# First attention of a fused cross-attention kernel: four pools become six, in another order

## The chip, the cores and the metric

The kernel runs on one core of one Trainium2 chip. The metric is the device time of one execution in microseconds (us), lower is better. A core has five instruction streams that matter here: TensorE (PE, matrix products; its weight loads are listed apart as PEld), VectorE (DVE), ScalarE (ACT), GpSimd (POOL) and SyncE (SP), which issues the DMAs. Each stream is executed in the order in which it was written when the program was built; between streams there are only semaphores.

## The reference, cut to what matters

`x` is (8, 112, 512), the context `ctx` (8, 375, 512), all float32. Four layers follow each other on `x`:

```
layer 0:  q = x Wq^T; k = ctx Wk^T; v = ctx Wv^T
          x = x + alpha * (softmax(q k^T / sqrt(512)) v) Wo^T
layer 1:  RWKV block: layer norm, token shift, mixing, a scan over time, group norm, gate, channel mix
layer 2:  a second RWKV block
layer 3:  two cross attentions to ctx with 16 heads of 128 and a 2048-wide GELU MLP, layer norm before each
```

The values of the third layer, `ctx wv`, depend on `ctx` and weights only. Nothing of layers 0 to 2 enters them.

## The kernel before

All activations lie with channels on the 128 partitions: `x` is one tile of 128 x 4 x 896. The program is written with a tile framework. A **pool** is a range of on-chip memory with a stack discipline: pools opened later lie above those still open, and a pool opened after others were closed takes their place from the bottom. What is put into a new pool waits until the pools that lay at its addresses are done with. PSUM, the accumulators of PE, consists of eight banks and is handed out by the same stack. The order of the instructions on each engine is made at build time by a list scheduler: it takes the instructions in the order of the program, and where the next one of an engine is not ready by its own estimate of the times, it puts a later one that is ready first. Only the time loop of the RWKV layers has an order written out by hand.

**Layer 0 (`layer0`, from line 224).** The weights are folded: `w_qk` is made from `w_q` and `w_k` (`turned`, `product`, L305), `q0 = x w_qk` is projected for all tokens (L308), and `w_vo` is made from `w_v` and `w_o` (L315). Then a loop over the eight batches (L316): `context(b)` loads the transposed context tile `cx` (24 KB-per-partition slots for four of them); `park` (L248, every second batch) makes sums and differences of two contexts and stores them to DRAM as `blocks`; `rows` are transposes of `cx` by `ident` (L327); scores `sc` (L333), softmax, transposed probabilities `pt` (L337), and `av` (L343), copied to the tile `z` (L346). At the end one projection, `z` by `w_vo`, is added to `x` (L348 to L352; PE at L161, the eviction `add` on DVE at L350, out of two PSUM banks).

Its pools, bottom first: `a0` (`keep`: `ident`, three `turned` tiles, `w_qk`, `q0`, `z0`, `w_vo`), `a0w` (`work`: `cx`, `blocks`, `rows`, small tiles), and in PSUM `a0p` (`ps`: two banks `mm`, for all projections and transposes of rows) and `a0s` (`ps2`: two banks each of `sc`, `pt`, `av`).

**What comes after.** When layer 0 closes its pools, these are opened, bottom first: `values` (L1429; seven weight tiles `wv`, five context blocks `cv`, six result tiles `k`, two more), `mmp` in PSUM (two banks), `rc` with a short-lived `rs` above it (constants of the RWKV layers: `heads`, `same`, `ident_rs`, `ones_t`, `pick`, L796 to L815), then `r1` and `m1` (first RWKV layer, with six PSUM banks `mp1`). In bytes per partition, worked out from the shapes: `values` 54 KB, `rc` with `rs` 4 KB, `r1` 56 KB, `m1` 30 KB; in layer 0, `ident` 0.5, `turned` 24, `w_qk` 8, `q0` 14, `z0` 14, `w_vo` 8, `cx` 23.4 KB.

**The filler.** `values()` (L820) is a generator of PE work that depends on nothing in the RWKV layers: the values of layer 3, by a seven-product scheme (k1, k6, k7, k2, k8 and two late ones, k5 and k9). Each product is two matmuls of 128 x 512, which the profile lists as four records (`ps_vk`, L906); ACT copies the bank out (L931, L999, L1013), POOL adds for three of the seven (L932), SP stores to DRAM. The first call (`fill(1)`, L1434) issues the loads: four of `cv` (L890), four of `wv` (L839), biases (L950, L951), and four sums of `wv` on POOL (L846 to L849). Later calls of `fill(n)` in the RWKV layers each place n products. Before the time loop of the first RWKV layer these are 3 + 2 + 2 + 2 + 2 inside `mixes(0, ...)` and 8 in `time_mix`.

**The first layer norm of layer 1** (`layer_norm_half`, L166, half 0 of the tokens): partial sums on DVE (`part_mean_ln`, L178, L180), a PE product with a constant matrix (`mean_ln`, L182), the subtraction (`xa`, L187, DVE), squares (L189, ACT), partial sums (`part_var_ln`), PE (`var_ln`, L182), the root (L194, ACT), the reciprocal (L195, DVE), the scaling (L196, DVE; L202, ACT), then the token shift on POOL (`sx`, L359, L360), `xx` on DVE (L438) and the first product of the layer, `ps_t` (L447, PE).

Of the kernel before, what the change touches and what calls it, by code (L numbers as in the profile page):

```python
# [22 lines left out]
F32 = mybir.dt.float32  # L23
# [3 lines left out]
PSUM = bass.MemoryType.PSUM  # L27
ORDERED = {mybir.EngineType.PE, mybir.EngineType.DVE, mybir.EngineType.Activation, mybir.EngineType.Pool}

P = 128  # L30
B, L, C, S = 8, 112, 512, 375
N = B * L
NC = C // P
# [75 lines left out]
def tile_kernel(ctx: ExitStack, tc: tile.TileContext, d: dict, out: bass.AP):  # L109
# [14 lines left out]
    def weight(name, g=None):  # L124

        w = wpool.tile([P, NC, C], F32, tag="w", name=f"w_{name}_{g}")
        nc.sync.dma_start(w, d[name] if g is None else d[name][g])
        return w
# [23 lines left out]
    def mm(ps, name):  # L152
        return ps.tile([P, 512], F32, tag="mm", name=name)

    def project(ps, w, rhs, evacuate, name, hs=(0, 1), os=range(NC)):

        for h in hs:
            for o in os:
                p = mm(ps, f"ps_{name}_{o}_{h}")[:, :NH]
                for k in range(NC):  # L160
                    nc.tensor.matmul(  # L161
                        p, w[:, k, o * P : (o + 1) * P], rhs(k, h), start=k == 0, stop=k == NC - 1
                    )
                evacuate(o, h, p)
# [59 lines left out]
    def layer0():  # L224

        with (
            tc.tile_pool(name="a0", bufs=1) as keep,
            tc.tile_pool(name="a0w", bufs=2) as work,  # L230
            tc.tile_pool(name="a0p", bufs=2, space=PSUM) as ps,
            tc.tile_pool(name="a0s", bufs=2, space=PSUM) as ps2,
        ):
            ident = identity(keep, "a0")
            w_q, w_k = weight("L0_xattn_w_q"), weight("L0_xattn_w_k")
            nc.sync.dma_start(x, d["xT"])
            cxs = {}

            def context(b):
                cxs[b] = work.tile([P, NC, S], F32, tag="cx", name=f"cx0_{b}", bufs=4)  # L240
                nc.sync.dma_start(cxs[b], d["ctxT"][:, b])

            context(0)
            w_v, w_o = weight("L0_xattn_w_v"), weight("L0_xattn_w_o")
            nc.sync.dma_start(alpha, d["alpha"].to_broadcast([P, 1]))
# [37 lines left out]
            def turned(w, name):  # L283

                t = keep.tile([P, NC, C], F32, tag="turned", bufs=3, name=f"t_{name}")
                for o in range(NC):
                    p = mm(ps, f"ps_t{name}_{o}")
                    for k in range(NC):
                        nc.tensor.transpose(p[:, k * P : (k + 1) * P], w[:, k, o * P : (o + 1) * P], ident)
                    (nc.vector.tensor_copy if o % 2 else nc.scalar.copy)(t[:, o, :], p)  # L290
                return t

            def product(a, b, name, scale=1.0):

                y = keep.tile([P, NC, C], F32, tag=name, name=name)
                for c in range(NC):
                    p = mm(ps, f"ps_{name}_{c}")
                    for k in range(NC):
                        nc.tensor.matmul(
                            p, a[:, k, c * P : (c + 1) * P], b[:, k, :], start=k == 0, stop=k == NC - 1  # L300
                        )
                    nc.scalar.activation(y[:, c, :], p, AF.Copy, scale=scale)
                return y

            w_qk = product(turned(w_q, "q"), turned(w_k, "k"), "w_qk", 1.0 / math.sqrt(C))  # L305
            q = keep.tile([P, NC, N], F32, name="q0")
            z = keep.tile([P, NC, N], F32, name="z0")
            project(  # L308
                ps,
                w_qk,  # L310
# [1 line left out]
                lambda o, h, p: nc.scalar.copy(halves(q[:, o, :], h), p),  # L312
                "q0",
            )
            w_vo = product(turned(w_v, "v"), w_o, "w_vo")  # L315
            for b in range(B):  # L316
                tok = slice(b * L, (b + 1) * L)
                if b + 1 < B:
                    context(b + 1)
                cx = cxs[b]  # L320
# [1105 lines left out]
    shared["spill"] = ctx.enter_context(tc.tile_pool(name="spill", bufs=1, space=bass.MemoryType.DRAM))  # L1426
    shared["blocks"] = shared["spill"].tile([P, (UNITS + 3) * BLOCKS * BLOCK], F32, name="blocks")
    layer0()
    with (  # L1429
        tc.tile_pool(name="values", bufs=1) as shared["pool"],  # L1430
# [80 lines left out]
```

## Time and profile before

| | us |
|---|---|
| median of 3 runs | 2971.14 (2968.95 to 2975.28) |
| the profiled execution, its own time | 2968.51 |
| its span on the core | 2966.1 |
| PE busy | 2861.6 (96% of the span) |
| DVE busy | 1610.9 (54%) |
| ACT busy | 998.9 (34%) |
| POOL busy | 876.4 (30%) |
| mean granted clock of PE | 0.988 of full speed |

A line of the timeline is: start in us, duration, engine, line of the program, operation, output <- inputs, and in brackets how long the engine had been idle before it and what released it. A line of the chain is: start, duration, engine, what and line; the chain is followed back from the last instruction to what released each step, and "issue" is time in which the engine waited for nothing that the profile shows. A line of the stages is: from:to, length, then busy time and number of instructions of PE, PEld, DVE, ACT and POOL, the granted clock of PE as a share of full speed, the busy share of the DMA engines and the GB/s that they moved. "SPq" is SP's queue of DMA issues.

### The profile page before, as it was taken

What the parts mean: (1) busy time and instruction counts of PE and PEld (TensorE: products, weight loads), DVE (VectorE), ACT (ScalarE), POOL (GpSimd) and SP (SyncE); (2) the same over time, 40 slices, a digit from 0 to 9 for tenths busy, and PEclk for the clock granted to TensorE, in tenths of its full rate; (3) what the DMA queues carried; (4) which work ended last, traced back from release to release, by engine and by line L of the source; (5) the groups of instructions that cost most, each with busy time, mean ns of one, the idle gap of its engine ahead of it and who ended that gap; (6) DMA issues with size and microseconds to landing.
All of it is one profiled execution on the core that took longest, in us unless ns stands there. A gap on an engine that the chain in (4) does not pass through costs nothing.

```text
span 2966.1 us, 29798 instructions
## 1 busy us (share of the span) xinstructions
PE 2861.6 (96%) x10130; PEld 1561.7 (53%) x10130; DVE 1610.9 (54%) x2350; ACT 998.9 (34%) x1992; POOL 876.4 (30%) x702
## 2 busy tenths in 40 slices
PE   8979999999999999999899999999999999999999
PEld 4734443344444433356465666666565656656544
DVE  1563288857342688743455554545554554545455
ACT  2123355533233555532332323232331323323311
POOL 2142078754231588732411010100302010000030
PEclk9989999999999999999999999999999999999999
DMA  6421398944321889742344344334233433432110
GB/s 255 150 89 45 116 291 247 282 135 126 96 68 54 246 251 271 225 141 70 130 130 128 129 128 129 108 119 140 88 120 102 144 108 119 140 114 77 42 54 25
DMA packets 199318, 402.90 MB, mean 136 GB/s; under 512 B 33288, under 2 KB 119592, under 8 KB 192384
## 3 DMA queue, kind: packets, MB, share of 16 engines
q1 hardware_dynamic: 199168, 401.01, 43.0%
q8 instruction: 81, 1.33, 0.2%
q14 instruction: 69, 0.57, 0.1%
HBM read 323.16 MB, written 77.91 MB: 135 GB/s over the span
## 4 chain that ended last, share of the span: by engine, by line
PE 80%; DVE 7%; POOL 4%; issue 3%; ACT 3%; DMA 2%; SPq 0%; DVEq 0%; POOLq 0%; ACTq 0%
PE ps_vk L906 13%; PE ps_k1k L1134 10%; PE ps_k5k L1134 7%; PE av L1303 6%; PE sc L1290 5%; PE ps_o L161 3%; PE pt L1293 3%; PE ps_fk L161 2%; PE ps_k1q L1061 2%; PE ps_k L484 2%; PE ps_r L484 2%; PE ps_k5q L1061 2%; PE ps_k7q L1061 2%; PE ps_fr L161 2%; PE ps_k5o L1061 1%
## 5 line engine op out<-in xcount | busy, mean ns | idle before, releaser
L906 PE MATMUL ps_vk<-wv,cv 128*128 128x512 f32 x1328 | 597.0, 600 | 29.5 <-DMA wv<-in_L_xattn_wv 8.2
L906 PEld LDWEIGHTS ps_vk<-wv,cv 128*128 128x128 f32 x1328 | 249.3, 191 | 361.7 <-issue 301.8
L932 POOL TENSOR_TENSOR k<-k,k 128x512 f32<-128x512 f32 (+1 forms) x153 | 201.7, 1318 | 306.7 <-ACT k L931 261.6
L691 DVE TENSOR_TENSOR_SCAN st<-decay,kv 128x904 f32<-128x904 f32 x128 | 260.7, 2037 | 16.7 <-POOL rs L695 4.0
L695 POOL TENSOR_TENSOR rs<-st,r 128x896 f32<-128x896 f32 x128 | 246.7, 1928 | 55.3 <-DVE st L691 42.4
L218 ACT ACTIVATE prob<-sc,top 112x376 f32<-112x376 f32 (+1 forms) x264 | 151.8, 575 | 322.6 <-DVE top L215 195.2
L1303 PEld LDWEIGHTS av<-pts,v 125*128 125x128 f32 (+1 forms) x1536 | 185.7, 193 | 31.0 <-DVE pts L1299 16.0
L1290 PE MATMUL sc<-k,q 128*112 128x376 f32 x512 | 201.1, 485 | 0.7 <-ACT prob L218 0.7
L1283 POOL COPY k<-over_k 128x4 f32<-128x4 f32 x64 | 13.8, 224 | 604.7 <-PE sc L1290 576.7
L1303 PE MATMUL av<-pts,v 125*128 125x112 f32 (+1 forms) x1536 | 190.0, 278 | 1.8 <-DVE pts L1299 0.9
L1134 PE MATMUL ps_k1k<-cs,wsk 128*128 128x375 f32 x480 | 178.6, 481 | 1.5 <-ACT p1k L1137 1.5
L215 DVE TENSOR_REDUCE top<-sc 112x1 f32<-112x376 f32 (+1 forms) x264 | 143.5, 545 | 64.3 <-PE sc L1290 51.9
L687 DVE TENSOR_TENSOR kv<-vp,k 128x904 f32<-128x904 f32 x128 | 141.5, 1105 | 64.8 <-ACT vp L589 59.0
L931 ACT COPY k<-ps_vk 128x512 f32<-128x512 f32 (+1 forms) x153 | 89.2, 583 | 183.1 <-PE ps_vk L906 180.2
L999 ACT COPY k<-ps_vk 128x512 f32<-128x512 f32 (+1 forms) x153 | 89.1, 582 | 153.6 <-PE ps_vk L906 148.7
L1293 PEld LDWEIGHTS pt<-ident_l,prob 112*125 112x125 f32 (+1 forms) x768 | 97.8, 176 | 72.0 <-DVE prob L220 43.9
L1293 PE MATMUL pt<-ident_l,prob 112*125 112x112 f32 (+1 forms) x768 | 121.4, 277 | 2.5 <-DVE prob L220 1.9
L220 DVE TENSOR_SCALAR prob<-prob,total 112x376 f32<-112x376 f32 (+1 forms) x264 | 118.3, 448 | 8.0
L1134 PEld LDWEIGHTS ps_k1k<-cs,wsk 128*128 128x128 f32 x480 | 89.5, 190 | 59.4 <-ACT p1k L1137 1.8
L589 ACT COPY vp<-vj 128x896 f32<-128x896 f32 x124 | 112.8, 910 | 7.0 <-DMA vj<-rows 3.1
L1141 DVE TENSOR_TENSOR k<-ps_k5k,u2k 128x375 f32<-128x375 f32 x52 | 28.5, 548 | 159.2 <-PE ps_k5k L1134 158.2
L1310 DVE TENSOR_TENSOR ctxt<-av,bv 128x448 f32<-128x448 f32 x64 | 39.9, 624 | 128.8 <-PE av L1303 128.8
(384 smaller groups left out, 4800.6 us busy)
## 6 DMA issues: line engine op xcount, KB each, us to landing
vj<-rows SPq DMA_DIRECT2D x124, 448.0 KB
cv<-blocks SPq DMA_DIRECT2D x181, 251.5 KB
cs<-blocks SPq DMA_DIRECT2D x120, 375.0 KB
wvs<-k SPq DMA_DIRECT2D x128, 256.0 KB
v<-wvs SPq DMA_DIRECT2D x64, 512.0 KB
cx<-in_ctxT SPq DMA_DIRECT2D x38, 750.0 KB
v<-wvs SPq DMA_DIRECT2D x64, 252.0 KB
wvs<-k SPq DMA_DIRECT2D x64, 224.0 KB
```

The source lines that it names most:

```text
L161: nc.tensor.matmul(p, w[:, k, o * P : (o + 1) * P], rhs(k, h), start=k == 0, stop=k == NC - 1)
L215: nc.vector.tensor_reduce(top, scores, AX.X, ALU.max, negate=True)
L218: nc.scalar.activation(prob, scores, AF.Exp, bias=top, accum_out=total)
L691: nc.vector.tensor_tensor_scan(flat(st), flat(decay[:, c]), flat(kv), 0.0, ALU.mult, ALU.add)
L695: nc.gpsimd.tensor_mul(by_batch(rs), st[:, :, :L], by_batch(r[:, c, :]))
L906: nc.tensor.matmul(to, left, right, start=start and n == 0, stop=k == 1, skip_group_check=True)
L932: nc.gpsimd.tensor_add(y, z, y)
L1061: nc.tensor.matmul(to, lhsT, rhs, start=start and k == 0, stop=k == 1, skip_group_check=not start)
L1134: nc.tensor.matmul(y, lhsT, rhs, start=start and k == 0, stop=k == 1, skip_group_check=True)
L1290: nc.tensor.matmul(sc, q[:, o, tok], kt[:, o, :], start=True, stop=True)
L1293: nc.tensor.transpose(pt[t][:nt, o, :], prob[:, t0 : t0 + nt], ident[:L, :L])
L1303: nc.tensor.matmul(av[:, o, :], v[:nt, t, o * HD : (o + 1) * HD], pts[:nt, t, o, :], start=t == 0, stop=t == 2,)
```

## The change

Layer 0 takes six pools instead of four, and their order changes. The context tiles `cx` leave `work` for a pool of their own, `a0c` (`near`), which is opened before `keep`. `z0` and `w_vo` leave `keep` for a pool `a0z` (`last`), opened after `keep`. In PSUM the pool with `sc`, `pt` and `av` (`a0s`) is opened first, the one with the two `mm` banks (`a0p`) last. `product` gets the pool as an argument. No instruction is added, removed or given other operands than other addresses.

```diff
         with (
+
+            tc.tile_pool(name="a0s", bufs=2, space=PSUM) as ps2,
+            tc.tile_pool(name="a0c", bufs=4) as near,
             tc.tile_pool(name="a0", bufs=1) as keep,
+            tc.tile_pool(name="a0z", bufs=1) as last,
             tc.tile_pool(name="a0w", bufs=2) as work,
             tc.tile_pool(name="a0p", bufs=2, space=PSUM) as ps,
-            tc.tile_pool(name="a0s", bufs=2, space=PSUM) as ps2,
         ):
...
-                cxs[b] = work.tile([P, NC, S], F32, tag="cx", name=f"cx0_{b}", bufs=4)
+                cxs[b] = near.tile([P, NC, S], F32, tag="cx", name=f"cx0_{b}")
...
-            def product(a, b, name, scale=1.0):
+            def product(a, b, name, pool, scale=1.0):
 
-                y = keep.tile([P, NC, C], F32, tag=name, name=name)
+                y = pool.tile([P, NC, C], F32, tag=name, name=name)
...
-            w_qk = product(turned(w_q, "q"), turned(w_k, "k"), "w_qk", 1.0 / math.sqrt(C))
+            w_qk = product(turned(w_q, "q"), turned(w_k, "k"), "w_qk", keep, 1.0 / math.sqrt(C))
             q = keep.tile([P, NC, N], F32, name="q0")
-            z = keep.tile([P, NC, N], F32, name="z0")
+            z = last.tile([P, NC, N], F32, name="z0")
...
-            w_vo = product(turned(w_v, "v"), w_o, "w_vo")
+            w_vo = product(turned(w_v, "v"), w_o, "w_vo", last)
```

## The prediction

> **What bounds the kernel now.** The page says PE 96% busy, so time is to be had only where PE waits. I read the busy time by stage first, cut at the end of layer 0's last projection, at the landing of the values' weights and at the first product of layer 1.
>
> ```profile
> core 0: us, PE busy (x) PEld busy (x) DVE busy (x) ACT busy (x) POOL busy (x), PEclk, DMA share, GB/s
> 134.00:146.00 12.00, 12.00 (x34) 6.09 (x33) 3.82 (x6) 0.53 (x1) 0.00 (x0) 1.00 0.56 133
> ...
> 158.30:166.40 8.10, 0.02 (x1) 0.06 (x1) 3.90 (x4) 1.70 (x1) 0.00 (x0) 0.66 0.94 293
> 166.40:176.00 9.60, 7.28 (x11) 3.00 (x12) 5.98 (x4) 2.98 (x4) 8.10 (x4) 0.75 0.40 136
> 176.00:186.40 10.40, 6.87 (x17) 2.55 (x15) 8.51 (x12) 4.77 (x9) 6.14 (x9) 0.93 0.39 126
> ```
>
> For 8.1 us PE does nothing and the DMA engines are 94% busy; just before, in the last projection, PE is full and POOL idle. The same question put to 186.4 to 260 and 260 to 390 gives PE 68.5 of 73.6 and 128.5 of 130 us: after the gap PE is the bound again.
>
> Then who waited for whom, from 140 to 190 us:
>
> ```profile
> POOL ident_rs masks.py:197 <- PE ps_o L161: 48.5, 1, 48.5
> ...
> PE ps_vk L906 <- DMA wv<-in_L_xattn_wv: 8.2, 1, 8.2
> ...
> PE ps_t L447 <- DVE xx L438: 3.5, 1, 3.5
> ...
> PE ps_vk L906 <- POOL wv L848: 2.3, 1, 2.3
> ```
>
> The three PE lines add to 14.0 us, all of PE's waiting here. Why the loads are late, SP's queue says:
>
> ```profile
> 142.94 0.63 SPq L409 DMA_DIRECT2D d<-in_L_xattn_decay_w  x1
> 157.54 1.79 SPq L890 DMA_DIRECT2D cv<-blocks  x4
> 159.38 2.64 SPq L839 DMA_DIRECT2D wv<-in_L_xattn_wv  x4
> ```
>
> SP is idle for 14 us and starts when the projection's last product ends (157.47). By the sizes `cv` lies at 28 to 38 KB, over `w_qk` and `q0`, last read at 127.6 by the scores. So the wait is for the whole pool `keep`, whose `z0` and `w_vo` are read to the end. Last the chain of waits (130 to 190 us):
>
> ```profile
> 134.16 23.33 PE ps_o L161 x62
> ...
> 159.38 6.91 DMA wv<-in_L_xattn_wv
> ...
> 166.38 2.05 PE ps_vk L906 x2
> 168.42 1.51 PE var_ln L182 x2
> ...
> 170.61 2.67 DVE part_mean_ln L180
> ...
> 175.88 2.94 DVE rstd__ln L195
> ...
> 181.04 1.94 DVE xa L196
> ...
> 186.35 4.10 PE ps_t L447 x5
> ```
>
> The layer norm's `var_ln` stands in PE's order behind a value product that waits for its weights; then DVE is late for the reciprocal.
>
> **What the change does to the waits.** `near` (23.4 KB) and `keep` without `z0` and `w_vo` (46.5 KB) are 69.9 KB; `values` with `rc` and `rs` takes 58 KB and lies inside them. Their last reader is the last transpose of `pt` by `ident`, ending at 130.6. So the values' loads, their POOL sums and the constants of the RWKV layers can start at about 131 instead of 157.5. In PSUM, by the stack, the values' two banks now lie over `sc`, free by then, and the layer norm's six over `pt`, `av` and the projection's two `mm` banks.
>
> **Part by part**, on the profiled execution.
>
> *Loads.* From the first issue at 157.54 to the last sum's operands 10 us passed (POOL starts at 167.66). Issued at 131 they land near 141, or up to 9 us later, at 150, if the 1.5 MB of layer 1's own loads (issued 134.6 to 143.6, which is their 9 us) come between. The 18 issues of this group (4 `cv`, 4 `wv`, 4 biases, 1 `heads`, 4 `same`, 1 `first`) take SP 10.5 us. They move ahead of or between layer 1's 14 small loads, which are wanted by `ps_t`, 30 us later: nothing.
>
> *`var_ln`.* Its input is ready at 162.86 + 1.28 = 164.14, it starts at 168.22: 4.08 us. Its two records take 1.70 us at the low clock after the idle stretch, 0.92 for `mean_ln`: 0.78 us.
>
> *Reciprocal.* Its input is ready at 171.29 + 0.63 = 171.92, it starts at 175.88: 3.96 us. In between DVE does two sums for half 1 (L180), 2.65 us each instead of 0.62 at 162.86, while POOL does the sums of `wv`. With POOL's sums gone they take 1.3 us, in the shadow of the root.
>
> *Small work in DVE's order.* The reciprocal ends at 178.82, `xa` starts at 180.97, behind L952, L804 and L813, which need late loads: 2.15 us. They go into the projection, where DVE is busy 3.5 to 3.8 of 12 us.
>
> *A new wait.* `mean_ln` (157.31 before) takes a bank of a pool that now covers the `mm` banks; if it waits for the last eviction (L350, 157.51 to 158.19), as the pool-wide wait above suggests, it ends at 159.1 instead of 158.2. Behind it on PE stand value products that can as well be put before it; DVE's `xa` waits. Between 0 and 0.9 us; I take 0.9, since SP's wait was of that kind.
>
> The sum: 4.08 + 0.78 + 3.96 + 2.15 - 0.9 = 10.1 us earlier for `ps_t`: 176.3. Step by step: `mean_ln` to 159.1, `xa` to 161.3, squares to 163.0, sums to 165.0, `var_ln` to 166.0, table and root to 168.0, reciprocal to 170.95, `xa` to 172.95, and 3.4 us to `ps_t` as before (182.97 to 186.35).
>
> *The gap as room for products.* From 158.2 to 176.3 are 18.1 us, less 1.84 for the two norm products 16.3. The six products (24 records) that ran there took 11.0 us at full clock (start to start 0.456 us, 16 in 7.30) and fit. Of the other 5.3 us the scheduler may fill up to two more products of 1.8 us, if ACT, which has the squares, the root and 0.58 us a copy to do, keeps up: 0 to 3.6, I take 1.8. It counts, since PE is the bound afterwards. Against it, a product may stand before `var_ln` when that is ready: 0 to 1.8, I take 0.9. Together 10.1 + 1.8 - 0.9 = **11 us**.
>
> *POOL's sums beside the projection.* Their 10.3 us now lie at about 141 to 152, beside evictions (L350) that must keep pace with PE: 2.94 us a bank, two banks. Here a rule speaks against the change: the Trainium skill, "SBUF — State Buffer", section "Who interferes with whom", says that a DVE instruction with two SBUF inputs and a GpSimd instruction that reads SBUF lock each other out for a whole instruction. The L180 row agrees (2.65 against 0.62). Counting `alpha` as the second SBUF input, each of four evictions would lose about 2 us, 8 in all less a bank's slack of 2.9: 5 us. But L459 has that form (PSUM, a column, an SBUF operand) and takes 0.67 us at 204.4 to 206.2 with POOL busy throughout. So only the three `part_mean` sums are blocked, at most 2 us each, one per bank time: 0.68 + 2.65 = 3.3 us against 2.94, which the spare bank absorbs. I take 0; bounds 0 to 5.
>
> *All else* is the same instructions in the same layer: nothing. What could still move is the written order further down, since the scheduler sees other ready times. The trace can't price that; the nearest row for a bad guess is the 8.2 us wait for `wv`. I give it no sign and keep 3 us either way in the range.
>
> The median is 2.6 us above the profiled execution (2971.14, 2968.51); I take the gain off the median: 2971.1 - 11 = 2960.
>
> **The rivals.** What a measurement of this kernel can tell from no change is 0.2%, 5.9 us: 2965.2 to 2977.1.
>
> *A, the forecast:* gap closed as summed. 2953 to 2965; chance 0.66.
>
> *B, half given back:* POOL's sums do hold up evictions (5 us), or products stand before both norm products (up to 2 x 1.8): 11 - 5 = 6, or with both 2. 2965 to 2969; chance 0.16. For it speaks the L180 row; against it L459.
>
> *C, it doesn't do what it says:* some instruction still ties `near` or `keep` to the end of the projection. Then nothing moves: 2971, within 3. Against: every reader of `cx`, `q0` and `ident` that the trace shows ends by 130.6. Chance 0.07.
>
> *D, slower:* a value product is written into PE's order inside the projection, before its weights have landed. For it: in the trace of before PE stood at `ps_vk` from 158.23 and the weights came at 166.38, so the order assumed them at least 8 us too early. Issued at 131 beside layer 1's loads they land as late as 150; PE standing from 139 to 150 would lose 11 us, the whole gain, and the products done there no longer fill the layer norm's gap: five of them at 1.8 are 9 us. So -11 + 11 + 9: 2980. With the gap left empty it is slower than before from a wait of 2 us on, by over 0.2% from 8. Against it: PE has the projection's products ready and full from 134 (12.00 of 12.00), and these come first in the program. Chance 0.11.
>
> **The numbers.** Faster by over 0.2%: A but for its edge, and half of B: 0.72. Within: the rest of B, C and some of D: 0.18. Slower: 0.10. Range 2953 to 2969: A and B, 0.82.
>
> **What would show it.** SP's `cv` and `wv` issues at 131 to 135; POOL L846 to L849 before 155 with PE's `ps_o` still in 23.5 us (else B); no wait of PE for DMA `wv`; L180 at 0.62; `ps_t` at 176 and the granted clock near 1 from 158 to 176. I am wrong if the issues stay at 157, if `ps_o` stretches, or if `ps_t` comes 10 us earlier and the end does not: then a later stage has its own bound.

## The result and the profile after

| | before | after |
|---|---|---|
| median of 7 runs each, us | 2970.40 (2966.97 to 2975.28) | 2961.31 (2951.97 to 2963.65) |
| ratio, 95% interval | | 0.9968 (0.9957 to 0.9979) |
| profiled execution, its own time, us | 2968.51 | 2963.03 |
| its span, us | 2966.1 | 2961.2 |

The change is 9.1 us faster by the medians; 2960 was forecast. In a second set on one chip (22 runs of the change, 49 of before) it was 2959.85 against 2967.23, ratio 0.9982 (0.9972 to 0.9992). By the ratios, which are not quotients of the medians, the gain is 9.5 us (6 to 13) in the first set and 5.3 us (2 to 8) in the second. That it is faster is clear; its size is known to some us only, since single runs of one kernel spread over 15 us and more (2959.99 to 2978.88 for before in that set).

SP's queue in the changed kernel (lines from L300 on stand 3 higher):

```profile
132.81 2.02 SPq L893 DMA_DIRECT2D cv<-blocks  x4
134.89 2.25 SPq L842 DMA_DIRECT2D wv<-in_L_xattn_wv  x4
...
154.88 0.64 SPq L398 DMA_DIRECT2D maa<-in_L_xattn_maa_w  x1
```

The loads leave when the last transpose of `pt` ends, 25 us earlier than before, and layer 1's own loads now come after them. PE's timeline from there to the first product of layer 1:

```profile
132.56 0.93 PE L161 MATMUL ps_o<-z,w_vo 128*128 128x448 f32 x2
133.42 2.90 PE L346 MATMUL av<-pts,rows 125*128 125x112 f32 x24
136.16 14.46 PE L161 MATMUL ps_o<-z,w_vo 128*128 128x448 f32 x38
153.93 9.29 PE L161 MATMUL ps_o<-z,w_vo 128*128 128x448 f32 x24 [3.31 <-DVE x L353]
163.05 1.02 PE L909 MATMUL ps_vk<-wv,cv 128*128 128x512 f32 x2
163.99 1.02 PE L182 MATMUL mean_ln<-part_mean_ln,mean_c 128*128 128x448 f32 x2
164.84 6.48 PE L909 MATMUL ps_vk<-wv,cv 128*128 128x512 f32 x14
171.16 0.92 PE L182 MATMUL var_ln<-part_var_ln,mean_c 128*128 128x448 f32 x2
172.00 9.71 PE L909 MATMUL ps_vk<-wv,cv 128*128 128x512 f32 x22
182.99 1.02 PE L450 MATMUL ps_t<-xx,maa 128*128 128x448 f32 x2 [1.28 <-DVE xx L441]
```

The layer norm's gap is almost full of value products, with no wait for DMA; the only stand left is 1.28 us for `xx`. But inside the last projection there is a new stand: PE waits 3.31 us for an eviction. Where it comes from, DVE's and POOL's timelines of the same stretch show:

```profile
142.26 2.35 POOL L849 TENSOR_TENSOR wv<-wv,wv 128x1024 f32<-128x1024 f32 x1 [8.84 <-DMA wv<-in_L_xattn_wv]
142.35 2.73 DVE L178 TENSOR_TENSOR part_mean_ln<-x 128x448 f32<-128x448 f32 x1
144.69 2.61 POOL L850 TENSOR_TENSOR wv<-wv,wv 128x1024 f32<-128x1024 f32 x1
145.01 0.67 DVE L353 SCALAR_TENSOR_TENSOR x<-ps_o,alpha,x 128x448 f32<-128x448 f32 x1
145.72 2.06 DVE L180 TENSOR_TENSOR part_mean_ln<-part_mean_ln,x 128x448 f32<-128x448 f32 x1
147.37 2.62 POOL L851 TENSOR_TENSOR wv<-wv,wv 128x1024 f32<-128x1024 f32 x1
147.70 5.58 DVE L955 TENSOR_TENSOR over<-over,bv 4x512 f32<-4x512 f32 x2
150.07 2.67 POOL L852 TENSOR_TENSOR wv<-wv,wv 128x1024 f32<-128x1024 f32 x1
...
153.20 0.67 DVE L353 SCALAR_TENSOR_TENSOR x<-ps_o,alpha,x 128x448 f32<-128x448 f32 x1
```

Before, with POOL idle in the projection, the same partial sums and, later, the same bias differences took:

```profile
140.19 0.63 DVE L178 TENSOR_TENSOR part_mean_ln<-x 128x448 f32<-128x448 f32 x1
143.20 0.62 DVE L180 TENSOR_TENSOR part_mean_ln<-part_mean_ln,x 128x448 f32<-128x448 f32 x1
178.74 1.78 DVE L952 TENSOR_TENSOR over<-over,bv 4x512 f32<-4x512 f32 x2
```

The eviction itself takes 0.67 us at 145.01 with POOL busy. The work with two inputs in on-chip memory that stands ahead of it in DVE's order is what POOL holds up: two partial sums take 2.73 and 2.06 us in place of 0.63 and 0.62, and the two bias differences 5.58 us in place of 1.78. Experiment 5 tests this. The stages, cut at these points:

```profile
136.00:150.60 14.60, 14.60 (x41) 7.21 (x40) 9.58 (x7) 0.53 (x1) 8.10 (x4) 1.00 0.54 183
150.60:154.00 3.40, 0.09 (x2) 0.08 (x1) 3.40 (x4) 0.00 (x0) 2.13 (x1) 1.00 0.06 12
...
163.20:171.20 8.00, 8.00 (x20) 3.06 (x19) 4.58 (x5) 3.36 (x4) 1.19 (x3) 1.00 0.56 150
171.20:183.00 11.80, 10.52 (x26) 4.26 (x24) 8.08 (x6) 8.07 (x13) 5.20 (x7) 1.00 0.45 133
```

PE is full in the layer norm's first 8 us, the stretch in which it had done nothing, and the granted clock is 1.00 throughout.

Since layer 0 reaches the projection at another time in every run (129.1 to 134.6 us among the profiled ones, 2.2 us later here than before), the steps below are compared from the projection's first product on PE. From there, in us:

| | before | after | after, second trace |
|---|---|---|---|
| `mean_ln` starts | 26.91 | 31.43 | 30.98 |
| `var_ln` starts | 37.82 | 38.60 | 38.15 |
| `ps_t` starts | 55.95 | 50.43 | 49.98 |
| records of value products before `ps_t` | 24 | 38 | 38 |
| first group norm in the time loop (`ps_gm`) | 311.38 | 300.00 | 299.59 |
| first query product of layer 3 (`ps_k1q`) | 1344.23 | 1337.21 | 1334.83 |

The gain at `ps_gm` is 11.4 and 11.8 us. Of it 5.5 and 6.0 are an earlier `ps_t`. The rest lies behind `ps_t`: up to `ps_gm` 190 records of value products are left in place of 204 (228 in all from the projection on, in both kernels), and that stretch takes 249.6 us in both traces of the change in place of 255.4. The 14 records done earlier account for it, at 0.44 us each (22 in 9.71).

### The profile page after: what moved, and what is told of

Read it like the earlier page. It is cut to its first block, busy times and chain, and to the rows that moved or that the text cites. A ratio compares the mean times of both kernels' runs of the same rounds, so it can differ in the third digit from the quotient of the medians.

```text
span 2961.2 us, 29809 instructions
## 1 busy us (share of the span) xinstructions
PE 2862.5 (97%) x10130; PEld 1563.9 (53%) x10130; DVE 1610.6 (54%) x2350; ACT 998.8 (34%) x1992; POOL 876.7 (30%) x702
## 4 chain that ended last, share of the span: by engine, by line
PE 80%; DVE 8%; POOL 4%; issue 3%; ACT 3%; DMA 2%; SPq 0%; DVEq 0%; POOLq 0%; ACTq 0%
PE ps_vk L909 13%; PE ps_k1k L1137 10%; PE ps_k5k L1137 7%; PE av L1306 6%; PE sc L1293 5%; PE ps_o L161 3%; PE pt L1296 3%; DVE st L694 2%; PE ps_fk L161 2%; PE ps_k1q L1064 2%; PE ps_r L487 2%; PE ps_k L487 2%; PE ps_fr L161 2%; PE ps_k5q L1064 2%; PE ps_k7q L1064 2%
## 5 line engine op out<-in xcount | busy, mean ns | idle before, releaser
L1002 ACT COPY k<-ps_vk 128x512 f32<-128x512 f32 (+1 forms) x153 | 89.1, 582 | 169.2 <-PE ps_vk L909 146.4
```

## The experiments

They were timed in three sets, each beside the kernel before on one chip; the median of before tells the set. The times, with the medians in us:

| | runs | this | before | ratio, 95% interval |
|---|---|---|---|---|
| on-chip pools only | 11 | 2960.22 | 2967.87 | 0.9971 (0.9961 to 0.9982) |
| PSUM pools only | 13 | 2968.37 | 2967.87 | 1.0001 (0.9993 to 1.0009) |
| contexts left in `work` | 14 | 2968.02 | 2967.87 | 0.9997 (0.9987 to 1.0008) |
| change, biases on POOL | 5 | 2958.12 | 2967.87 | 0.9964 (0.9952 to 0.9976) |
| change, sums on DVE | 5 | 2956.55 | 2968.39 | 0.9959 (0.9943 to 0.9975) |
| change, sums on DVE, biases on POOL | 17 | 2957.59 | 2968.39 | 0.9971 (0.9961 to 0.9980) |
| on-chip pools, sums on DVE | 5 | 2954.56 | 2968.39 | 0.9953 (0.9940 to 0.9966) |
| the change again | 22 | 2959.85 | 2967.23 | 0.9982 (0.9972 to 0.9992) |
| before, sums on DVE | 19 | 2964.03 | 2967.23 | 0.9985 (0.9975 to 0.9995) |
| on-chip pools, sums on DVE, again | 15 | 2958.86 | 2967.23 | 0.9972 (0.9961 to 0.9983) |

An interval is about 3 us to each side, so the versions that gain are not told apart by their times. Where they differ, the traces decide what happened.

**1. Which pools carry the gain?** On-chip pools of the change, PSUM pools in the old order:

```diff
-            tc.tile_pool(name="a0s", bufs=2, space=PSUM) as ps2,
             tc.tile_pool(name="a0c", bufs=4) as near,
...
             tc.tile_pool(name="a0p", bufs=2, space=PSUM) as ps,
+            tc.tile_pool(name="a0s", bufs=2, space=PSUM) as ps2,
```

> Only the on-chip pools are changed; the PSUM pools stand in the old order, so the values' first products still need the banks of the last projection and start at its last eviction, about 0.7 us after its end, while the layer norm's banks are free at once. Theory (the gain is the earlier loads, the PSUM order only decides by about 1 us who stands first after the projection): 8 to 12 us under before, the same as the change within 2 us; mean_ln directly behind the projection. Rival (the products need their banks before the projection ends to fill the gap): at most half the change's gain, 3 to 6 us under before.

It gains 7.7 us by the medians and 5 to 12 by the ratio, as the change does: a little under the theory, over the 3 to 6 us of the rival, whose upper end the interval doesn't quite exclude. Its `mean_ln` follows the projection without a wait for the last eviction, and 34 records come before `ps_t` where the change has 38. Its `ps_gm` is 7.2 us earlier than before, where the change has 11.4 and 11.8; the trace shows a reason for this that is not the PSUM order. After PE's stand in the projection (2.86 us here) the granted clock stayed at half for almost 6 us:

```profile
151.30:157.00 5.70, 5.70 (x8) 2.83 (x9) 1.89 (x8) 0.31 (x1) 0.00 (x0) 0.50 0.57 147
```

The projection's last 24 records took 12.29 us there and 9.29 us in the change, whose clock stayed at 1.00 after stands of 3.31 and 2.85 us. What decides between the two, no run here shows. Experiment 7 repeats the comparison without such a stand.

**2.** The reverse, PSUM pools alone:

```diff
+            tc.tile_pool(name="a0s", bufs=2, space=PSUM) as ps2,
             tc.tile_pool(name="a0", bufs=1) as keep,
...
-            tc.tile_pool(name="a0s", bufs=2, space=PSUM) as ps2,
```

> Only the PSUM pools are changed; on-chip pools as before. Theory: the loads still leave at the end of the projection, so nothing is gained; mean_ln waits about 0.9 us for the last eviction: 0 to 1 us over before, not to be told from it. Rival (free banks for the values are what gives the gain): 5 us or more under before.

No difference in time, as expected. PE's timeline shows both halves of the expectation, the small new wait for the last eviction and the old one for the weights:

```profile
159.29 1.02 PE L182 MATMUL mean_ln<-part_mean_ln,mean_c 128*128 128x448 f32 x2 [0.78 <-DVE x L350]
167.01 2.07 PE L906 MATMUL ps_vk<-wv,cv 128*128 128x512 f32 x2 [6.70 <-DMA wv<-in_L_xattn_wv]
```

**3. Pool or tile?** The change with the contexts left in `work`, so that `values` reaches into `z0`:

```diff
-            tc.tile_pool(name="a0c", bufs=4) as near,
...
-                cxs[b] = near.tile([P, NC, S], F32, tag="cx", name=f"cx0_{b}")
+                cxs[b] = work.tile([P, NC, S], F32, tag="cx", name=f"cx0_{b}", bufs=4)
```

> The change with the contexts left in the work pool, so that the pool below z0 and w_vo holds 46.5 KB and the values' 54 KB reach some 8 KB into z0. Theory (what is loaded first waits for every pool that its own pool touches): the loads leave at the end of the projection again and the gain is gone; 0 to 2 us over before. Rival (each tile waits only for what lies at its own bytes; the first weights and context blocks lie below z0): the loads leave at about 131 and the gain stays, 7 to 12 us under before.

The gain is gone, as the theory had it. SP's queue in it:

```profile
158.69 1.79 SPq L892 DMA_DIRECT2D cv<-blocks  x4
160.52 2.04 SPq L841 DMA_DIRECT2D wv<-in_L_xattn_wv  x4
```

A separate pool for `z0` and `w_vo` is not enough. The pools below it must hold the whole of what is opened next, here 54 KB of `values`; 46.5 do not, although the first loads lie below `z0`. The waits are by pool.

**4. What stretches the projection?** First the two bias differences on POOL, where they come behind the sums:

```diff
-            nc.vector.tensor_sub(over, over, bv)
+            nc.gpsimd.tensor_sub(over, over, bv)
```

> The change with the two small bias differences (4 x 512) computed on POOL, not on DVE. In the change's trace these two held DVE for 5.6 us behind POOL's weight sums and PE stood 3.3 us in the projection. Theory (that hold is what stretched the projection): the projection takes about 23.5 us again and the time is 2 to 4 us under the change, 11 to 14 under before. Rival (the blocked partial sums of the layer norm hold the evictions up just as long): the same as the change within 1 us, PE's stand stays at 2 us or more.

The theory fell: PE still stands 2.8 us in the projection, in two pieces (0.91 and 1.88), and `mean_ln` starts 32.87 us after the projection's first product (31.43 in the change). About 2 us of this is the clock: after the second stand it was 0.62 and then 0.50 of full speed up to 163 us, and the last eight records of the projection took 4.97 us, not 3. The stand itself the trace shows as a hold passed on. The biases now wait on POOL behind the sums, their stores on SP wait for them, three of the four small loads `same` stand behind those stores, and DVE stands for ACT's `mean_h` with two evictions behind it:

```profile
158.37 0.29 DVE L812 TENSOR_TENSOR less_mean_h<-ident_rs,mean_h 128x128 f32<-128x128 f32 x1 [4.26 <-ACT mean_h L811]
158.58 0.68 DVE L353 SCALAR_TENSOR_TENSOR x<-ps_o,alpha,x 128x448 f32<-128x448 f32 x1
```

**5.** So take the supposed cause away: the four sums of the first weight set on DVE, so that POOL runs nothing beside the projection but two short instructions at its start:

```diff
-            nc.gpsimd.tensor_sub(s2, a11, a21)
-            nc.gpsimd.tensor_add(a21, a21, a22)
-            nc.gpsimd.tensor_sub(s1, a21, a11)
-            nc.gpsimd.tensor_sub(s3, a12, s1)
+            eng = nc.gpsimd if at else nc.vector
+            eng.tensor_sub(s2, a11, a21)
+            eng.tensor_add(a21, a21, a22)
+            eng.tensor_sub(s1, a21, a11)
+            eng.tensor_sub(s3, a12, s1)
```

> The change with the four sums of the first set of values' weights on DVE, not on POOL, so that POOL reads nothing beside the projection. Theory (POOL's sums lock DVE's two-input work out and so hold up the evictions; moving the bias differences alone did not help because the waits went to the next DVE work): part_mean back at 0.62 us, the bias differences under 1 us each, the projection in 23.5 to 25 us, not 27 to 29; 2 to 4 us under the change, 11 to 14 under before. Rival (DVE now stands in its order for the weights' DMA and needs about 4.6 us for the sums itself, and the projection stretches just as long): the same as the change within 1.5 us.

DVE's timeline in it:

```profile
141.43 1.23 DVE L850 TENSOR_TENSOR wv<-wv,wv 128x1024 f32<-128x1024 f32 x1 [3.30 <-DMA wv<-in_L_xattn_wv]
142.57 0.68 DVE L353 SCALAR_TENSOR_TENSOR x<-ps_o,alpha,x 128x448 f32<-128x448 f32 x1
143.16 1.22 DVE L851 TENSOR_TENSOR wv<-wv,wv 128x1024 f32<-128x1024 f32 x1
144.29 0.62 DVE L178 TENSOR_TENSOR part_mean_ln<-x 128x448 f32<-128x448 f32 x1
...
147.69 0.67 DVE L956 TENSOR_TENSOR over<-over,bv 4x512 f32<-4x512 f32 x1
```

The theory held: everything is back at its own length (each bias difference at 0.67 us), the sums take 4.9 us on DVE against 10.3 on POOL, and PE's stand in the projection is 0.21 us. DVE does wait 3.30 us in its order for the weights, and one spare bank covers it. `mean_ln` starts at 28.46, `ps_t` at 47.44, 2.5 to 3 us before the change's. By the median it gains 11.8 us; the mechanism is shown by the trace, a gain over the change by the times is not.

**6.** Both moves together:

> The same, and the two bias differences on POOL. Theory: DVE has nothing but evictions, partial sums and the four weight sums to do; the projection takes 23.5 to 25 us and the time equals that of the sums on DVE within 1 us. Rival (what still holds DVE is waiting for ACT's mean_h behind late small loads): the projection keeps a stand of PE of 1.5 us or more and the time is no better than the change.

The biases on POOL (2.88 us for the two, from 141.81) now lock out one partial sum (L178, 1.70 us) and one weight sum (L852, 2.28 us on DVE), and PE stands 2.33 us; `mean_ln` starts at 30.42:

```profile
141.88 1.70 DVE L178 TENSOR_TENSOR part_mean_ln<-x 128x448 f32<-128x448 f32 x1
143.49 2.28 DVE L852 TENSOR_TENSOR wv<-wv,wv 128x1024 f32<-128x1024 f32 x1
```

Neither text had that: even two small POOL operations bring the stand back. DVE has no wait for `mean_h` here, so the rival's cause is out, though its stand of PE came true.

**7.** The sums on DVE with the old PSUM order (experiments 1 and 5 together):

> The sums on DVE with the on-chip pools of the change and the PSUM pools in the old order. Theory (the PSUM order only decides who stands first behind the projection): within 2 us of the sums on DVE with the new PSUM order. Rival (without the late stretch of the projection the free banks count: products can start before the last eviction): 3 us or more over it.

The theory held: 2954.56 against 2956.55. PE:

```profile
133.75 23.09 PE L161 MATMUL ps_o<-z,w_vo 128*128 128x448 f32 x61
156.68 0.92 PE L182 MATMUL mean_ln<-part_mean_ln,mean_c 128*128 128x448 f32 x2
```

The projection is as short as before the change, `mean_ln` stands directly behind it (26.91), and `ps_t` starts at 46.85.

**8.** On one more chip, the change again, to see whether its profiled loss near layer 3 returns:

> The change itself once more, on the same chip as the next two. Theory (the trace of its profiled run lost 4.7 us in the 150 us around the start of layer 3, in stretches of low granted clock that other runs with the same order do not show): 8 to 12 us under before, and a second trace without that loss in layer 3. Rival (the early products are missing later and the time is given back there): the same 3 to 5 us loss between the second channel mix and the first query product again.

It doesn't: from the first key product of layer 3 (`ps_k1k`) to `ps_k1q` before takes 38.5 us, the first trace of the change 41.5 and the second 39.2. In the first, the clock granted from 1420 to 1450 us was 0.77, against 0.89 before (0.83 in the second). So it is not at layer 3 that a gain is regularly given back. But of the 11.8 us at `ps_gm` only 9.4 are left at `ps_k1q`. One step of it, about 1.65 us, lies around layer 2's channel mix in both traces (between `ps_fk` and `ps_fr` in the first, between `ps_o` and `ps_fk` in the second). The PSUM-only kernel, which gains nothing, has the same step, and experiments 3 and 9 have not; experiment 7 has 0.5 us of it, the others have it once and the trace of experiment 10 twice. So an early start is not its cause, and its cause stays open. The median gain, 7.4 us, came in a little under the 8 to 12 expected.

**9.** The kernel before with nothing but the sums on DVE:

> The kernel before with only the four sums of the first weight set on DVE in place of POOL; loads as late as before. Theory (the reciprocal's 4 us delay comes from the sums standing in the layer norm's time at all): the partial sums take 0.62 us again, but DVE has 4.9 us of weight sums in its own order there, so the first product of layer 1 is moved by less than 2 us and the time is the same within 2 us. Rival (the lock between POOL and DVE alone is worth its 4 us): 3 to 5 us under before.

Half right. As the theory had it, the reciprocal is no earlier (175.95; 175.88 before) and `ps_t` moves by 1.7 us only, measured from the projection. Yet it gains 3.2 us by the medians, the size the rival named, on another path:

```profile
166.10 2.05 PE L907 MATMUL ps_vk<-wv,cv 128*128 128x512 f32 x2 [8.23 <-DMA wv<-in_L_xattn_wv]
167.94 1.70 PE L182 MATMUL var_ln<-part_var_ln,mean_c 128*128 128x448 f32 x2
169.44 10.30 PE L907 MATMUL ps_vk<-wv,cv 128*128 128x512 f32 x22
```

With sums of 1.2 in place of 2.6 us PE no longer waits 2.3 us for the third one, and six more records (30 against 24; the last six follow at 180.41) fit ahead of `ps_t`. The 8.2 us for the weights stay; of the versions here only those with the earlier loads are without them.

**10.** And the best version again, beside the change:

> The on-chip pools of the change, PSUM pools in the old order, and the four sums on DVE, on the same chip as the change. Theory (the projection in 23.5 us and mean_ln directly behind it are worth 3 to 5 us on top of the change): 12 to 15 us under before and 3 to 5 under the change. Rival (the difference seen so far is between chips or chance): within 1.5 us of the change.

By the medians the rival came true: 8.4 us under before, not 12 to 15, and 1 us under the change. By the ratios it is 3 us under the change (0.9972 against 0.9982), with overlapping intervals. Its trace repeats that of experiment 7 up to the layer norm (`mean_ln` at 27.31, `ps_t` at 47.26). But the 2.5 to 3.5 us by which `ps_t` is earlier than the change's in experiments 5, 7 and 10 are not all kept: `ps_gm` starts at 298.34, 298.21 and 297.78 (300.00 and 299.59 in the change), and `ps_k1q` at 1335.08, 1335.10 and 1336.11, between or near the change's 1337.21 and 1334.83. So taking the stand away is worth 1 to 2 us up to the time loop, and neither the traces nor the times show that more than this arrives at the end.

## Why the prediction was right, step by step

*The cause.* The waits are by pool, and it is the on-chip pools that matter: experiments 1 to 3 show it by taking each part alone. Rival C (nothing moves) is what experiment 3 looks like; rival D (a product inside the projection that waits for weights) did not occur. What rival B feared did: POOL's sums held evictions up, though not in the way B had it, through `alpha`.

*Loads.* First issue to POOL's first sum: 9.45 us (132.81 to 142.26), 10 predicted. Layer 1's loads went 20 us later, behind the stores of the biases, and no PE wait for them appears.

*`var_ln`.* Input ready at 169.49 + 1.29 = 170.78, start 171.16: 0.38 us late where 0.9 was taken, 0.92 us long where it had been 1.70. Held.

*Reciprocal and small work.* Ready at 173.89, start at 173.97; ends at 176.91, `xa` at 176.95. Both delays are gone as summed, 3.96 us but for 0.08, and 2.15 us.

*The new wait.* `mean_ln` at 163.99, after the last eviction, which ends at 163.93; predicted 0.9, and a product's first two records stand ahead of it as foreseen. Experiment 1 shows the order without it.

*From `xa` to `ps_t`.* Taken as 3.4 us, measured 182.99 - 178.97 = 4.02 us. A copy of a value product (L1002, 179.17) stands ahead of ACT's scaling.

*POOL's sums beside the projection: the step that was mis-sized.* I took 0 within 0 to 5. It was 3.3 us of PE, and `mean_ln` came 3.6 later than the 27.8 of the forecast. The rule of the Trainium skill, "SBUF — State Buffer", section "Who interferes with whom", that a DVE instruction with two SBUF inputs contends with a GpSimd instruction that reads SBUF, was applied rightly to the evictions, 0.67 us beside a busy POOL, and to the partial sums, 2.73 and 2.06 us. What I left out were the bias differences: I moved them into the projection for nothing as "small work in DVE's order", without asking that rule about them. They have two SBUF inputs too, and with both 4 x 512 operations behind POOL's sums they cost 5.58 us, more than the spare bank holds. Experiments 5 and 7 show the stand gone with the sums off POOL (0.21 us and none), experiment 4 that moving the biases alone only passes it on.

*Room for products: mis-sized the other way.* I allowed two more products, 3.6 us, and took 1.8; it was 14 more records, 3.5 products, 6 us. I had priced records at 0.456 us start to start from a stretch with waits for ACT's copies in it (16 in 7.30); here 22 take 9.71, 0.44. And by the same timeline the gap from the last `ps_o` to `ps_t` is 19.8 us (163.22 to 182.99), longer than the 18.1 worked out.

So the sum, 11 us, was met by two misses that cancel: 5.5 us from an earlier `ps_t`, not 10.1, and 6 us from products, not 0.9 net. At `ps_gm` the trace has 11.4 us. The cause, the earlier loads, was right; that the sum agrees is luck. The prediction's own signs say the same: the loads, the clock and the missing wait for DMA came as named, but `ps_o` stretched, which it had named as a sign of being wrong, two partial sums took over 2 us where 0.62 was named, and `ps_t` came 5.5 us earlier and not 10. What arrives in the median is 7 to 9 us. Both traces of the change lose 1.65 us at layer 2's channel mix, for a cause that stays open, and the first another 3 us at layer 3's start, under a lower granted clock; what the unprofiled runs lose, no trace shows. One suspect was not tried: in the two traces of the change layer 0 itself reaches the projection 2.2 and 4.2 us later than in that of before. PE stood 4.2 us in both ahead of the second half of `w_vo` (3.0 before), and the granted clock from 62 to 76 us was 0.76 (0.88 before). But the other kernels scatter too (129.1 to 132.2), experiment 1, with the same on-chip pools, reaches it at 130.4 as before does, and no instruction there was changed.

## What to carry to other kernels

In a stack of pools what a stage reads last belongs above everything that the next stage opens first, and the pools below must be big enough for all of it: here the wait was for whole pools, and an overlap of some 8 KB undid the whole gain. When loads are moved under another stage, list every instruction that they release, small ones too, and ask of each which engine's order it enters and what it locks there. Where work is always ready, as the value products are here, count an earlier start twice: the chain ends earlier (5.5 us), and the gap takes more of the work (14 records, 6 us).

## What the runs showed of the hardware

The lock between POOL and DVE stretched plain copies within SBUF as well: with the biases on POOL the copy L807 took 1.48 us (0.21 before) and the four of L816 2.63 us (0.46) while POOL's third and last sums ran. The same sums, 128 x 1024 with two SBUF inputs, take 1.22 us on DVE and 2.35 to 2.69 on POOL. After a stand of PE of about 3 us in the projection the granted clock was 1.00 in both traces of the change (3.31 and 2.85 us) and 0.50 for almost 6 us in that of experiment 1 (2.86 us), which cost the projection 3 us. And the mean granted clock of a run goes with its time: of the 49 runs of before in the last set those with 0.987 took 2970.6 us on average, those with 0.990 took 2963.9. So a few us between single traces mean nothing without it.
